# State-space stage of a five-layer model: decaying the state's part of y by rows of y, instead of scaling C for each head

## The chip, the cores and the metric

The kernel runs on one core of a Trainium2 chip. The metric is the device time of one execution in microseconds; the median of several runs is given. Everything is in float32.

## The reference, what matters of it

The model takes 1024 tokens of 512 features and adds six layers to them, one after the other, each behind a layer norm:

```python
x = x + 0.5 * ffn0(ln(x))        # 8 experts, top 2
x = x + attention(ln(x))         # 32 heads
x = x + 0.5 * ffn0(ln(x))
x = x + 0.5 * ffn1(ln(x))        # 4 routed LoRA adapters of rank 8
x = x + state_space(ln(x))       # the layer that is changed
x = x + 0.5 * ffn1(ln(x))
```

The state-space layer has 64 heads of 64 channels. The heads form 8 groups of 8; a group shares its vectors B and C of 128 elements (the state's width). From a projection of the input and a convolution over 4 tokens come x, B and C, from another projection the gate, and from a third the step dt of each head and token. Then, for each head (64 channels p, 128 state elements n):

```python
state = state * dA_t + (dt_t * x_t)[:, None] * B_t[None, :]   # dA = exp(-exp(A_log) * dt)
y_t   = state @ C_t
...
y  = y + x * D
yn = y * rsqrt(mean(y * y over the group's 512 channels) + eps) * norm_weight * silu(gate)
out = yn @ out_proj.T
```

## The kernel before, in words

The layers run one after another in one program. TensorE's (PE's) work is written out in program order; the tile framework adds semaphores and lets each engine (PE; VectorE, DVE; ScalarE, ACT; GpSimd, POOL; SyncE, SP, which issues most DMAs) run its own instructions in an order that it fixes when the program is built. [...] What buffers there are decides how far one engine can run ahead: `psml`, four PSUM tiles of one bank (`ps_y`, `ps_st`, `ps_tr`, `ps_ss`, `ps_out` and others take turns in it); `pbig`, two for the projections `ps_in`; in SBUF `ep`, two buffers of each of `dd`, `e_seg` and `cs`; `w2`, two of each of `xdt`, `xw`, `y`, `sq`, `yg`, `state`; `wpool`, four for weights.

The state-space layer is `mamba`. The scan over tokens is done in chunks of 128 tokens, 8 of them. First `steps_of_time` works out dt for every head and token (tiles `dt_e`, `dt_u` and so on, L1044 and L1047 among them), and writes two sets of rows to the DRAM tile `decay`: row 0 holds the decay dA of each token, row 1, `ecum`, the decay from the chunk's start to each token. SBUF tiles `erev` and `etot` hold the decay from each token to the chunk's end, and over the whole chunk.

Then come 16 units: 8 groups times two halves of 512 tokens, each half of four chunks. `load_group` loads a group's weights `w_bc`, `w_x`, `w_g` and `w_out`. For each chunk i of a unit the loop does, in program order:

1. `scan(un, i)`: this chunk's outputs and the new state.
2. projections for the **next** unit (`project_pair`, matmuls at L230): at i = 0 those of B, C and half of x (16 matmuls), at i = 1 the other half of x (8) and `finish_bc` (transposes of B, and `ps_bc` = C against B, masked to `gt`), at i = 2 and 3 the gate (8 each, `w_g`). The convolution of x, B and C takes six DVE instructions a tile, L1161 and L1170, so chunks 0 and 1 are DVE's heavy ones.
3. `prepare` for the next chunk.
4. `project_out` for this chunk.

`prepare` loads `dd`, two broadcasts of 1024 decay values (8 heads of 128 tokens) to all 128 partitions, 512 KB each. DVE makes from row 0 the decays between all pairs of tokens of a chunk by a scan (`e_seg`, L1265), and multiplies them by `gt` (L1273). PE transposes x (`ps_tr`, L156); DVE scales it by dt (`xdt`, L1278), and POOL that by `erev` (`xw`, L1284). For all chunks but a sequence's first (56 of 64), POOL also makes `cs`: C, which has the state's 128 elements on partitions, times row 1, for each of the 8 heads (128 x 1024, L1290).

`scan` forms `ps_y`, with the group's 512 channels as 4 blocks of 128 partitions by 128 tokens; a head's 64 channels are the lower or upper half of the partitions of a block. Eight matmuls with 64 columns of weights (`xdt` of one head) against `e_seg` of that head give the part from the chunk's own tokens, and eight more (the head's `state` against its `cs`) add the state's part in the same bank (both L1308). DVE adds `xd`, which is x times D (`y_m`, L1317). ACT squares y (`sq`, L1321), and DVE multiplies y by the gate (`yg`, L1323). The state goes on by `ps_st` (L1326), POOL's `state` times `etot` (L1333) and a DVE add (L1336). POOL adds the four blocks of squares in two steps (L1340, L1341), except in the last unit.

`project_out` sums the squares over partitions (`ps_ss`, L1349: one matmul, four in the last unit), makes the scale `ss` (L149 on DVE, L150 on POOL), multiplies `yg` by the output weights (`ps_out`, four matmuls, L1360), and adds that to x (L1363).

In the last group `after.step()` mixes in tiles of the last layer. In the last unit there are no projections left to stand between `scan` and `project_out`.

Of the kernel before, what the change touches and what calls it, by code (L numbers as in the profile page):

```python
# [13 lines left out]
F32 = mybir.dt.float32  # L14
# [4 lines left out]
ALU = mybir.AluOpType  # L19
# [3 lines left out]
P = 128  # L23
# [17 lines left out]
MP = 64  # L41
# [3 lines left out]
HPG = MH // MG  # L45
# [30 lines left out]
def macaron_kernel(  # L76
# [23 lines left out]
    nc = tc.nc  # L100
# [5 lines left out]
    psml = ctx.enter_context(tc.tile_pool(name="psml", bufs=4, space=PSUM))  # L106
# [6 lines left out]
    decay = [  # L113
        dram.tile([NCH // 2, 2, MH * P], F32, tag=f"decay{q}", name="decay")
        for q in range(2)
    ]
# [35 lines left out]
    def transposes(src, n):  # L152

        ps = psml.tile([P, 512], F32, tag="ps", name="ps_tr")
        for i in range(n):
            nc.tensor.transpose(ps[:, i * P : (i + 1) * P], src(i), ident)  # L156
        return ps
# [849 lines left out]
    def mamba(lora, par):  # L1007
        conv, dsk, nwt, w_dt, dtb, av = par.conv, par.dsk, par.nwt, par.w_dt, par.dtb, par.av
        nct = MI // P
        with ExitStack() as ms:  # L1010
# [13 lines left out]
            with tc.tile_pool(name="m_dt", bufs=1) as dp, tc.tile_pool(  # L1024
                name="m_pair", bufs=3
# [99 lines left out]
            w2 = ms.enter_context(tc.tile_pool(name="m_w2", bufs=2))  # L1125
            ep = ms.enter_context(tc.tile_pool(name="m_e", bufs=2))
            heads = [P, HPG, MP]

            def as_heads(a):
                return a.rearrange("p (h d) -> p h d", d=MP)  # L1130
# [51 lines left out]
            def begin_unit(gr, hf):  # L1182
                g = gr["g"]
                un = {"gr": gr, "hf": hf, "g": g, "last": (g, hf) == (MG - 1, 1)}
                un["bT"] = bp.tile([P, half], F32, tag="bT", name="bT")
                un["cT"] = bcp.tile([P, half], F32, tag="cT", name="cT")
                un["btok"] = bcp.tile([P, 4, P], F32, tag="btok", name="btok")
                un["gt"] = bcp.tile([P, 4, P], F32, tag="gt", name="gt")
                un["xc"] = bcp.tile([P, 4, half], F32, tag="xc", name="xc")
                un["xd"] = bcp.tile([P, 4, half], F32, tag="xd", name="xd")  # L1190
                un["sg"] = bcp.tile([P, 4, half], F32, tag="sg", name="sg")
                return un
# [56 lines left out]
            def per_head(a, un, i):  # L1249
                c, h0 = 4 * un["hf"] + i, un["g"] * HPG  # L1250
                return a[:, c, h0 : h0 + HPG].unsqueeze(2).to_broadcast(heads)

            def prepare(un, i):

                c, h0 = 4 * un["hf"] + i, un["g"] * HPG
                tok = slice(i * P, (i + 1) * P)
                dd = ep.tile([P, 2, HPG * P], F32, tag="dd", name="dd")
                for q in range(2):
                    nc.sync.dma_start(
                        dd[:, q, :],  # L1260
                        decay[un["hf"]][i, q, h0 * P : (h0 + HPG) * P].partition_broadcast(P),
                    )

                e = ep.tile([P, HPG, P], F32, tag="e", name="e_seg")
                nc.vector.tensor_tensor_scan(  # L1265
                    e.rearrange("p h l -> p (h l)"),
                    dd[:, 0, :],
                    eye8.rearrange("p h l -> p (h l)"),
                    0.0,
                    ALU.mult,  # L1270
                    ALU.add,
                )
                nc.vector.tensor_tensor(  # L1273
                    e, e, un["gt"][:, i, :].unsqueeze(1).to_broadcast([P, HPG, P]), ALU.mult
                )
                ps = transposes(lambda k: un["xc"][:, k, tok], 4)
                xdt = w2.tile([P, D], F32, tag="xdt", name="xdt")
                nc.vector.tensor_tensor(  # L1278
                    as_heads(xdt), as_heads(ps), per_head(dtp, un, i), ALU.mult
                )  # L1280
                xw = None
                if c < NCH - 1:
                    xw = w2.tile([P, D], F32, tag="xw", name="xw")
                    nc.gpsimd.tensor_tensor(  # L1284
                        as_heads(xw), as_heads(xdt), per_head(erev, un, i), ALU.mult
                    )
                cs = None
                if c > 0:
                    cs = ep.tile([P, HPG, P], F32, tag="cs", name="cs")
                    nc.gpsimd.tensor_tensor(  # L1290
                        cs,
                        un["cT"][:, tok].unsqueeze(1).to_broadcast([P, HPG, P]),
                        dd[:, 1, :].rearrange("p (h l) -> p h l", l=P),
                        ALU.mult,
                    )
                return e, xdt, xw, cs

            def scan(un, i, e, xdt, xw, cs):

                c, gr = 4 * un["hf"] + i, un["gr"]  # L1300
                tok = slice(i * P, (i + 1) * P)
                before = gr["state"]
                py = psml.tile([P, 512], F32, tag="ps", name="ps_y")
                terms = [(xdt, e)] + ([(before, cs)] if before is not None else [])
                for n, (left, right) in enumerate(terms):
                    for h in range(HPG):
                        r0 = (h % 2) * MP
                        nc.tensor.matmul(  # L1308
                            py[r0 : r0 + MP, (h // 2) * P : (h // 2 + 1) * P],
                            lhsT=left[:, h * MP : (h + 1) * MP],  # L1310
                            rhs=right[:, h, :],
                            start=(n == 0 and h < 2),
                            stop=True,
                            skip_group_check=not (n == 0 and h < 2),
                        )
                y = w2.tile([P, 4, P], F32, tag="y", name="y_m")
                nc.vector.tensor_tensor(  # L1317
                    y, py.rearrange("p (k l) -> p k l", l=P), un["xd"][:, :, tok], ALU.add
                )
                sq = w2.tile([P, 4, P], F32, tag="sq", name="sq")  # L1320
                nc.scalar.activation(sq, y, AF.Square)  # L1321
                yg = w2.tile([P, 4, P], F32, tag="yg", name="yg")
                nc.vector.tensor_tensor(yg, y, un["sg"][:, :, tok], ALU.mult)  # L1323
                if c < NCH - 1:
                    pst = psml.tile([P, 512], F32, tag="ps", name="ps_st")
                    nc.tensor.matmul(  # L1326
                        pst, lhsT=un["btok"][:, i, :], rhs=xw, start=True, stop=True
                    )
                    st = w2.tile([P, D], F32, tag="state", name="state")
                    if before is None:  # L1330
                        nc.vector.tensor_copy(st, pst)
                    else:
                        nc.gpsimd.tensor_tensor(  # L1333
                            as_heads(st), as_heads(before), per_head(etot, un, i), ALU.mult
                        )
                        nc.vector.tensor_tensor(st, st, pst, ALU.add)  # L1336
                    gr["state"] = st
                n = 4
                if not un["last"]:
                    nc.gpsimd.tensor_tensor(sq[:, :2, :], sq[:, :2, :], sq[:, 2:, :], ALU.add)  # L1340
                    nc.gpsimd.tensor_tensor(sq[:, 0, :], sq[:, 0, :], sq[:, 1, :], ALU.add)  # L1341
                    n = 1
                return un, c, yg, sq, n
# [26 lines left out]
            un = begin_unit(gr, 0)  # L1370
            for j in range(5):
                project_pair(un, j)
                if j == 1:
                    finish_bc(un)
            ready = prepare(un, 0)
            plan = ((0, 1), (2,), (3,), (4,))
            for n, _ in enumerate(units):
                nxt = None
                if n + 1 < len(units):
                    g, hf = units[n + 1]  # L1380
# [22 lines left out]
                un = nxt  # L1403
# [74 lines left out]
```

## Time and profile before

| | before |
|---|---|
| runs | 2933.84, 2933.5, 2931.63 us |
| median of the runs | 2933.5 us |
| profiled execution, own time | 2935.3 us |
| its span | 2933.6 us |
| mean granted TensorE clock | 0.978 |
| TensorE (PE) busy | 2800.9 us, 95% |
| VectorE (DVE) busy | 1745.8 us, 60% |
| GpSimd (POOL) busy | 898.8 us, 31% |
| ScalarE (ACT) busy | 709.4 us, 24% |
| `cs`, L1290, on POOL | 56 instructions, 184.2 us |

The span is that of the slowest (here the only) core in the profiled execution; its own time is a little longer, since it holds what lies around the span. Busy times of engines overlap, so they don't add up to the span. The state-space layer with what is mixed into it takes about the last third, from some 1876 to 2900 us. A line number stands for a line of the kernel before, unless it is said to be of the changed kernel.

### The profile page before, as it was taken

What the parts mean: (1) busy time and instruction counts of PE and PEld (TensorE: products, weight loads), DVE (VectorE), ACT (ScalarE), POOL (GpSimd) and SP (SyncE); (2) the same over time, 40 slices, a digit from 0 to 9 for tenths busy, and PEclk for the clock granted to TensorE, in tenths of its full rate; (3) what the DMA queues carried; (4) which work ended last, traced back from release to release, by engine and by line L of the source; (5) the groups of instructions that cost most, each with busy time, mean ns of one, the idle gap of its engine ahead of it and who ended that gap; (6) DMA issues with size and microseconds to landing.
All of it is one profiled execution on the core that took longest, in us unless ns stands there. A gap on an engine that the chain in (4) does not pass through costs nothing.

```text
span 2933.6 us, 30294 instructions
## 1 busy us (share of the span) xinstructions
PE 2800.9 (95%) x11051; PEld 1587.3 (54%) x11051; DVE 1745.8 (60%) x3239; ACT 709.4 (24%) x1381; POOL 898.8 (31%) x733
## 2 busy tenths in 40 slices
PE   5979999999999999999999769899999999999989
PEld 3435666656666666666654334454555555555544
DVE  3146555665656656556564234777776777767673
ACT  1212212231212222212222222422222232222320
POOL 4231112121122212112100230255554545455450
PEclk8989999999999999999999889999999999999999
DMA  8420001010010001001015340233232222223210
GB/s 297 126 72 29 15 15 44 1 44 15 15 44 15 29 15 43 15 15 43 1 36 194 101 122 18 83 101 108 86 108 94 86 98 97 93 87 122 87 44 29
DMA packets 102178, 196.99 MB, mean 67 GB/s; under 512 B 9040, under 2 KB 34800, under 8 KB 102032
## 3 DMA queue, kind: packets, MB, share of 16 engines
q1 hardware_dynamic: 84896, 157.15, 16.1%
q0 software_dynamic: 6240, 20.45, 2.7%
q10 hardware_dynamic: 10896, 17.47, 1.6%
q8 instruction: 89, 1.46, 0.2%
q14 instruction: 57, 0.47, 0.1%
HBM read 176.17 MB, written 18.87 MB: 66 GB/s over the span
## 4 chain that ended last, share of the span: by engine, by line
PE 84%; DVE 6%; POOL 4%; issue 3%; DMA 2%; ACT 0%; POOLq 0%; DVEq 0%; SPq 0%; ACTq 0%
PE ps_in L230 15%; PE ps_m L912 13%; PE ps_o L732 8%; PE ps_s L708 8%; PE ps_tr L156 7%; PE ps_out L1360 6%; PE ps_m L884 6%; PE ps_wo L821 6%; PE ps_e L510 5%; PE ps_y L1308 3%; PE ps_up L241 2%; PE ps_st L1326 1%; DVE xc L1161 1%; DVE e_seg L1265 1%; PE ps_v L241 1%
## 5 line engine op out<-in xcount | busy, mean ns | idle before, releaser
L708 PE MATMUL ps_s<-kT,qT 128*128 128x512 f32 (+3 forms) x768 | 292.8, 488 | 0.1
L732 PE MATMUL ps_o<-pT,v 128*128 128x512 f32 (+3 forms) x768 | 260.4, 489 | 0.0
L753 ACT COPY pT<-ps_tr 128x256 f32<-128x256 f32 (+2 forms) x192 | 91.7, 478 | 647.3 <-PE ps_tr L156 635.5
L722 ACT ACTIVATE pr<-ps_s,nm 128x128 f32<-128x128 f32 (+7 forms) x256 | 190.3, 744 | 238.3 <-DVE nm L719 207.9
L1360 PE MATMUL ps_out<-w_out,yg 128*128 128x512 f32 x512 | 241.1, 615 | 3.0 <-DVE yg L1323 3.0
L230 PE MATMUL ps_in<-hT,w_g 128*128 128x512 f32 x512 | 227.1, 596 | 8.2 <-issue 8.2
L1290 POOL TENSOR_TENSOR cs<-cT,dd 128x1024 f32<-128x1024 f32 x56 | 184.2, 3289 | 161.6 <-PE ps_y L1308 138.8
L230 PE MATMUL ps_in<-hT,w_x 128*128 128x512 f32 x512 | 225.8, 593 | 0.0
L732 PEld LDWEIGHTS ps_o<-pT,v 128*128 128x128 f32 x768 | 144.3, 191 | 145.6 <-issue 99.9
L719 DVE TENSOR_REDUCE nm<-ps_s 128x1 f32<-128x128 f32 (+7 forms) x256 | 192.2, 752 | 3.9
L156 PEld LDWEIGHTS ps_tr<-ident,pr 128*128 128x128 f32 x1152 | 136.9, 142 | 76.1 <-issue 44.8
L156 PE MATMUL ps_tr<-ident,pr 128*128 128x128 f32 x1152 | 171.4, 276 | 4.5 <-DVE pr L724 3.2
L510 PE MATMUL ps_e<-w_all,xt_s 128*128 (+1 forms) x368 | 168.1, 601 | 0.0
L724 DVE TENSOR_SCALAR pr<-pr,sm 128x128 f32<-128x128 f32 (+7 forms) x256 | 162.9, 637 | 7.7 <-DVE sm L723 0.5
L230 PEld LDWEIGHTS ps_in<-hT,w_g 128*128 128x128 f32 x512 | 96.6, 190 | 127.8 <-issue 127.8
L230 PEld LDWEIGHTS ps_in<-hT,w_x 128*128 128x128 f32 x512 | 97.0, 190 | 120.9 <-issue 120.4
L1265 DVE TENSOR_TENSOR_SCAN e_seg<-dd,eye 128x1024 f32<-128x1024 f32 x64 | 152.3, 2380 | 7.7 <-PE ps_y L1308 5.8
L1161 DVE SCALAR_TENSOR_TENSOR xc<-ps_in,conv,xc 128x511 f32<-128x511 f32 (+2 forms) x192 | 141.5, 737 | 17.9 <-ACT xc L1157 17.6
L708 PEld LDWEIGHTS ps_s<-kT,qT 128*128 128x128 f32 x768 | 127.5, 192 | 39.8 <-issue 26.8
L1360 PEld LDWEIGHTS ps_out<-w_out,yg 128*128 128x128 f32 x512 | 94.5, 195 | 98.4 <-issue 98.4
L806 POOL TENSOR_TENSOR so<-oT 128x256 f32<-128x256 f32 x28 | 20.0, 726 | 380.2 <-DVE oT L739 336.7
L1284 POOL TENSOR_TENSOR xw<-xdt,erev 128x512 f32<-128x512 f32 x56 | 58.4, 1043 | 251.6 <-DVE xdt L1278 195.0
(271 smaller groups left out, 4759.2 us busy)
## 6 DMA issues: line engine op xcount, KB each, us to landing
dd<-decay SPq DMA_DIRECT2D x128, 512.0 KB
w_all<-in_w_e_dram SPq DMA_DIRECT2D x16, 1024.0 KB
outs<-y_e ACTq DMA_DIRECT2D x46, 256.0 KB
w_v<-in_wkv_dram SPq DMA_DIRECT2D x8, 1024.0 KB
w_q<-in_wq_dram SPq DMA_DIRECT2D x32, 256.0 KB
w_k<-in_wkv_dram SPq DMA_DIRECT2D x8, 1024.0 KB
w_o<-in_wo_dram SPq DMA_DIRECT2D x8, 1024.0 KB
w_x<-in_in_wt_dram SPq DMA_DIRECT2D x8, 1024.0 KB
```

The source lines that it names most:

```text
L156: nc.tensor.transpose(ps[:, i * P : (i + 1) * P], src(i), ident)
L230: nc.tensor.matmul(ps[:, cols : cols + n], lhsT=w[:, k, c0 : c0 + P], rhs=hT[:, k, t0 : t0 + n], start=(k == 0), stop=(k == KT - 1),)
L510: nc.tensor.matmul(ps, lhsT=xt[:, k, :], rhs=w_all[:, bass.ds(ep, 1), k, :].rearrange("p e c -> p (e c)"), start=(k == 0), stop=(k == KT - 1),
L708: nc.tensor.matmul(ps[:, j : j + m], lhsT=qT[:, qt * P : (qt + 1) * P], rhs=kT[:, j : j + m], start=True, stop=True,)
L719: nc.vector.tensor_reduce(nm, ps[:, :n], AX.X, ALU.max, negate=True)
L722: nc.scalar.activation(pr[:, :n], ps[:, :n], AF.Exp, bias=nm, accum_out=sm)
L732: nc.tensor.matmul(ps[:, lo:512], lhsT=v[:, kb, hh * P : (hh + 1) * P], rhs=pT[:, kb, lo:512], start=(kb == 0), stop=(kb == last),)
L821: nc.tensor.matmul(ps[:, j, :], lhsT=lf[i][k][:, j * P : (j + 1) * P], rhs=rt[i][:, k, :], start=(first and j == 0 and k == 0), stop=(k == 1),
L912: nc.tensor.matmul(ps, lhsT=gr["left"][i][:, k, hh * P : (hh + 1) * P], rhs=right[i][:, k, :], start=(first and k == 0), stop=(last and k ...
L1265: nc.vector.tensor_tensor_scan(e.rearrange("p h l -> p (h l)"), dd[:, 0, :], eye8.rearrange("p h l -> p (h l)"), 0.0, ALU.mult, ALU.add,)
L1290: nc.gpsimd.tensor_tensor(cs, un["cT"][:, tok].unsqueeze(1).to_broadcast([P, HPG, P]), dd[:, 1, :].rearrange("p (h l) -> p h l", l=P), ALU ...
L1360: nc.tensor.matmul(po, lhsT=yg[:, k, :], rhs=w_o[:, k, :], start=(k == 0), stop=(k == 3))
```

## The change

A head's decay does not depend on the state's elements, so it can be applied to the result for each channel and token as well as to C. The changed kernel does that:

- `prepare` loads only row 0 into `dd`. For chunks behind a sequence's first, row 1 goes into a new tile `ec` of 128 partitions by 4 blocks by 128 tokens, laid out as y is: two broadcasts to 64 partitions, one for the even and one for the odd heads, 128 KB each in pieces of 512 bytes. `cs` and its POOL instruction are gone.
- `scan` forms the state's part by four matmuls with 128 columns of weights (`state` of two heads) against C itself, in a bank of its own, `ps_z` (L1318 of the changed kernel). DVE multiplies it by `ec` into a new tile `z_m` (L1326), POOL adds `xd` to that in place (L1329), and DVE adds `ps_y` and `z_m` (L1332). In a sequence's first chunk y is `ps_y` plus `xd`, as before.

```diff
-                dd = ep.tile([P, 2, HPG * P], F32, tag="dd", name="dd")
-                for q in range(2):
-                    nc.sync.dma_start(
-                        dd[:, q, :],
-                        decay[un["hf"]][i, q, h0 * P : (h0 + HPG) * P].partition_broadcast(P),
-                    )
+                dd = ep.tile([P, HPG * P], F32, tag="dd", name="dd")
+                nc.sync.dma_start(
+                    dd, decay[un["hf"]][i, 0, h0 * P : (h0 + HPG) * P].partition_broadcast(P)
+                )
+
+                ec = None
+                if c > 0:
+                    ec = ep.tile([P, 4, P], F32, tag="ec", name="ec")
+                    src = decay[un["hf"]][i, 1, h0 * P : (h0 + HPG) * P].rearrange(
+                        "(k r l) -> r k l", r=2, l=P
+                    )
+                    for r in range(2):
+                        nc.sync.dma_start(
+                            ec[r * MP : (r + 1) * MP, :, :], src[r].partition_broadcast(MP)
+                        )
...
-                cs = None
-                if c > 0:
-                    cs = ep.tile([P, HPG, P], F32, tag="cs", name="cs")
-                    nc.gpsimd.tensor_tensor(
-                        cs,
-                        un["cT"][:, tok].unsqueeze(1).to_broadcast([P, HPG, P]),
-                        dd[:, 1, :].rearrange("p (h l) -> p h l", l=P),
-                        ALU.mult,
-                    )
-                return e, xdt, xw, cs
...
                 py = psml.tile([P, 512], F32, tag="ps", name="ps_y")
-                terms = [(xdt, e)] + ([(before, cs)] if before is not None else [])
-                for n, (left, right) in enumerate(terms):
-                    for h in range(HPG):
-                        r0 = (h % 2) * MP
+                for h in range(HPG):
+                    r0 = (h % 2) * MP
+                    nc.tensor.matmul(
+                        py[r0 : r0 + MP, (h // 2) * P : (h // 2 + 1) * P],
+                        lhsT=xdt[:, h * MP : (h + 1) * MP],
+                        rhs=e[:, h, :],
+                        start=(h < 2),
+                        stop=True,
+                        skip_group_check=h >= 2,
+                    )
+                more = un["xd"][:, :, tok]
+                if before is not None:
+                    pz = psml.tile([P, 512], F32, tag="ps", name="ps_z")
+                    for k in range(4):
                         nc.tensor.matmul(
-                            py[r0 : r0 + MP, (h // 2) * P : (h // 2 + 1) * P],
-                            lhsT=left[:, h * MP : (h + 1) * MP],
-                            rhs=right[:, h, :],
-                            start=(n == 0 and h < 2),
+                            pz[:, k * P : (k + 1) * P],
+                            lhsT=before[:, k * P : (k + 1) * P],
+                            rhs=un["cT"][:, tok],
+                            start=True,
                             stop=True,
-                            skip_group_check=not (n == 0 and h < 2),
                         )
+                    z = w2.tile([P, 4, P], F32, tag="z", name="z_m")
+                    nc.vector.tensor_tensor(
+                        z, pz.rearrange("p (k l) -> p k l", l=P), ec, ALU.mult
+                    )
+                    nc.gpsimd.tensor_tensor(z, z, more, ALU.add)
+                    more = z
                 y = w2.tile([P, 4, P], F32, tag="y", name="y_m")
                 nc.vector.tensor_tensor(
-                    y, py.rearrange("p (k l) -> p k l", l=P), un["xd"][:, :, tok], ALU.add
+                    y, py.rearrange("p (k l) -> p k l", l=P), more, ALU.add
                 )
```

More of the change, by code (lines that the diff above doesn't have):

```diff
@@ L1266, in prepare @@
                     e.rearrange("p h l -> p (h l)"),
-                    dd[:, 0, :],
+                    dd,
                     eye8.rearrange("p h l -> p (h l)"),
@@ L1286, in prepare, with scan @@
                     )
-                cs = None
-                if c > 0:
-                    cs = ep.tile([P, HPG, P], F32, tag="cs", name="cs")
-                    nc.gpsimd.tensor_tensor(
-                        cs,
-                        un["cT"][:, tok].unsqueeze(1).to_broadcast([P, HPG, P]),
-                        dd[:, 1, :].rearrange("p (h l) -> p h l", l=P),
-                        ALU.mult,
-                    )
-                return e, xdt, xw, cs
-            def scan(un, i, e, xdt, xw, cs):
+                return e, xdt, xw, ec
+            def scan(un, i, e, xdt, xw, ec):
                 c, gr = 4 * un["hf"] + i, un["gr"]
```

## The prediction

> **What bounds the kernel now.** I read the profile page first (its span, its line of busy times, its groups), then the windows of the state-space stage, then PE's timeline for the order and the cadence of the matmuls, then the waits, and last the timelines of POOL and DVE at the places where PE waits.
>
> ```profile
> span 2933.6 us, 30294 instructions
> PE 2800.9 (95%) x11051; PEld 1587.3 (54%) x11051; DVE 1745.8 (60%) x3239; ACT 709.4 (24%) x1381; POOL 898.8 (31%) x733
> ...
> L1290 POOL TENSOR_TENSOR cs<-cT,dd 128x1024 f32<-128x1024 f32 x56 | 184.2, 3289 | 161.6 <-PE ps_y L1308 138.8
> ```
>
> TensorE is busy 95% of the span. The product `cs` that the change drops is the longest elementwise operation on POOL, 56 times 3.3 us, but POOL is busy for only 31%. The windows view (start and end, then sum and busy time of PE, PEld, DVE, ACT and POOL, granted clock, DMA share) of 200 us inside the state-space stage:
>
> ```profile
> 2200.00:2400.00 200.00, 199.37 (x842) 101.72 (x841) 142.49 (x196) 54.36 (x80) 98.32 (x67) 1.00 0.28 95
> ```
>
> PE idles 0.63 us in 200 us, at a granted clock of 1.00. So the 184 us of `cs` aren't on the path: the change can gain only where PE's own work shrinks, at the few places where PE waits, and at the edges of the stage.
>
> **PE's own work.** The timeline gives the starts (start, duration); the second pair is `finish_bc`, four 128x128 matmuls of 128 columns, the very shape of the new `ps_z`.
>
> ```profile
> 2307.59 1.09 PE L1308 MATMUL ps_y<-e_seg,xdt 128*64 128x128 f32 x16
> 2308.51 1.04 PE L1308 MATMUL ps_y<-cs,state 128*64 128x128 f32 x16
> 2309.48 1.13 PE L1326 MATMUL ps_st<-xw,btok 128*128 128x512 f32 x2
> 2310.45 1.02 PE L230 MATMUL ps_in<-hT,w_g 128*128 128x512 f32 x2
> ...
> 2352.45 1.06 PE L1239 MATMUL ps_bc<-cT,bT 128*128 128x128 f32 x8
> 2353.34 0.60 PE L156 MATMUL ps_tr<-ident,xc 128*128 128x128 f32 x4
> ```
>
> The state's part costs little for 8 matmuls: 0.97 us from its start to that of `ps_st` (the 64-wide ones run in pairs, one in each half of the array). From the start of `ps_y` to the next projection it is now 2310.45 − 2307.59 = 2.86 us. After: `ps_y` 0.92, or 1.02 where a 128-wide matmul follows (2003.05 to 2004.07 in a chunk without a state part); `ps_z` 2353.34 − 2352.45 = 0.89; `ps_st` 0.97, or 0.86 if the 0.1 for passing from 64 to 128 wide has been paid at `ps_z`. That makes 2.77 to 2.88. I take 2.83, −0.03 a chunk, over 56 chunks **−1.7 us** (bounds 56 × −0.09 = −5.0 and 56 × 0.01 = +0.6).
>
> **The places where PE waits.** The waits view (waiter, releaser: us, count, mean) names one steady wait inside the stage, and the timelines show it at the first two chunks of each group's conv half:
>
> ```profile
> PEld ps_ss L1349 <- POOL sq L1341: 8.0, 15, 0.6
> ```
> ```profile
> 2025.02 2.36 POOL L1290 TENSOR_TENSOR cs<-cT,dd 128x1024 f32<-128x1024 f32 x1 [1.51 <-PE ps_y L1308]
> ...
> 2025.65 1.74 DVE L1170 SCALAR_TENSOR_TENSOR xc<-hist,conv,xc 128x2 f32<-128x2 f32 x1
> ...
> 2028.10 0.68 DVE L1317 TENSOR_TENSOR y_m<-ps_y,xd 128x512 f32<-128x512 f32 x1
> ...
> 2030.84 2.70 POOL L1340 TENSOR_TENSOR sq<-sq 128x256 f32<-128x256 f32 x1
> 2033.62 1.32 POOL L1341 TENSOR_TENSOR sq<-sq 128x128 f32<-128x128 f32 x1
> 2035.00 0.38 PE L1349 MATMUL ps_ss<-ones,sq 128*128 128x1 f32 x2 [0.38 <-POOL sq L1341]
> ...
> 2046.93 2.02 POOL L1333 TENSOR_TENSOR state<-state,etot 128x512 f32<-128x512 f32 x1
> ...
> 2049.42 0.38 PE L1349 MATMUL ps_ss<-ones,sq 128*128 128x1 f32 x2 [0.24 <-POOL sq L1341]
> ```
>
> With the bubbles beside them, the two places cost 0.64 and 0.50 us of PE, 1.14 a group, 8.0 in seven groups (the eighth is mixed with the last FFN).
>
> Site one after: `cs` is gone, so the two-column L1170, 1.74 long here and 0.21 elsewhere, gives back 1.53. The new chain puts `z` (0.68, the price of L1317, which also reads PSUM), a hop of 0.09 (`xdt` to `xw`) and POOL's add (1.04, the price of `xw`, 128x512) ahead of `y`: 1.81. So `y` starts 0.28 later. `state×etot` (1.36 here) now starts when the add ends, 2028.4, and the squares' sums at 2029.8 instead of 2030.84; even at their long 2.70 + 1.32 they end by 2033.9, ahead of the 2034.62 at which PE would want them. The wait goes: −0.64.
>
> Site two after: here `y` (2044.21) is later by the full 1.81, so the squares (ACT, 0.63) are ready at about 2047.5. `cs` no longer stands before them, but `state×etot` (1.04 to 2.02) runs from 2046.0 to 2047.1 or 2048.0, and the sums (1.17 + 0.45 in this place) end at 2049.1 to 2049.7 against 2049.4 now. I take +0.15. Together −0.49 × 7 = **−3.5 us** (bounds: both waits gone, −8.0; site two at 2.5 times today's cost while site one stays, about +6). In the other chunks the sums end at 2315.70 where PE wants them at 2317.64, so 1.9 us are spare; `y` takes 1.1 of it, since `e*gt` (2.73 beside `cs`, 1.21 elsewhere) gives the rest back, and 0.8 is left. If that cover were gone, each 0.1 us beyond it would cost 3 us over some 30 chunks.
>
> **The start of the stage.** The two first `cs` run on POOL from 1843.09 to 1849.86, beside the chain that makes dt, while PE idles 8.21 us until 1855.85. The tile view of `dt_u` (count: min/mean/max ns):
>
> ```profile
> L1044 DVE TENSOR_SCALAR dt_u<-dt_e x2: 284/1009/1734, 1820.8 to 1845.9; 128x256 f32<-128x256 f32 x2
> ```
>
> One instance is 1.734 beside `cs` and 0.284 without; its neighbour L1047 has 1.770 and 0.293. That is −2.9 on an unbroken DVE chain. Against it, SP issues two `ec` transfers ahead of the first `dd`, 0.42 each, on which the first scan waits; the second 512 KB transfer is gone. I take **−2.5** (bounds −2.9 and +1). Later in the stage one 512 KB load gives way to two of 128 KB; a `dd` is asked for about a chunk ahead and the DMA engines are 28% busy, so I cost the extra 48 issues at nothing; a pair is 0.84 us on SP, and the weights and the next `dd` queued behind it hold PE up nowhere now (0.63 us idle of 200, above); should the cover be gone, it is up to 0.84 us for each of 56 chunks.
>
> **The tail.** In the last unit no projections cover `y`:
>
> ```profile
> 2875.50 0.69 DVE L1317 TENSOR_TENSOR y_m<-ps_y,xd 128x512 f32<-128x512 f32 x1 [1.99 <-PE ps_y L1308]
> ...
> 2876.91 1.05 PE L1349 MATMUL ps_ss<-ones,sq 128*128 128x1 f32 x8
> ```
>
> PE takes up the squares as soon as ACT has them. The chain of 1.81 is bare in its last two chunks, +3.6; in the first two `yg` loses a 2.73 us `e*gt` ahead of it and they come out even; the rest of group 7 I put at +0.5. Sum **+4.2** (bounds +2 and +7).
>
> **Sum.** −2.5 − 1.7 − 3.5 + 4.2 = −3.5. All durations are from one profiled execution of 2935.3 us (span 2933.6), 1.8 above the median of the runs, 2933.5; the sum makes it 2931.8, and the median 2930.0.
>
> [...] POOL's elementwise rows depend on the company: `state×etot` has 2.02 above and 1.04 in another chunk:
>
> ```profile
> 2316.06 1.04 POOL L1333 TENSOR_TENSOR state<-state,etot 128x512 f32<-128x512 f32 x1 [0.36 <-DVE state L1336]
> ```
>
> [...]
>
> **The rivals.** *Both waits go, and PE's part reaches its lower bound.* For it: the squares' sums lose `cs` as their neighbour everywhere. Then −2.9 − 5.0 − 8.0 + 4.2 = −11.7: 2921.8 us. Against it: site two's arithmetic above. Chance 0.29. *Slower: the add on POOL sits inside DVE's in-order queue.* `y` waits for it, and scan, `yg`, `e*gt` and the conv steps are queued behind `y`. If it takes 2.02, as `state×etot` did beside DVE work, instead of 1.04, that is 0.98 at 2 places in 7 groups, +13.7, and +2.0 in the tail, on −3.5: +12.2, 2945.7 us. An excess of 0.22 (a mean of 1.26) brings the sum to zero, one of 0.59 (1.63) to 5.9 slower. For it: the 2.02, 1.36 and 2.70 rows; against it: those met DVE operations on two SBUF tiles. Chance 0.28. *PE's part halves*, if eight matmuls become four at half the pair's cost: 56 × −0.44 = −24.6, 2909 us; against it the `ps_bc` row, 0.89 for just such four. Chance 0.03.
>
> **How the numbers follow.** 0.2%, 5.9 us, is about what a measurement of this kernel can tell from no change. The main case has 0.40, its own range 2926 to 2937: no change. Faster is the first rival and the third, 0.32; slower is the second, 0.28. The range takes in the first rival at 2921 and the second at 2947; outside stay the halved PE and the far sides of both.
>
> **What would show it.** Right: `ps_z` at 0.89 and 2.8 us from `ps_y` to the projection; L1044 and L1047 near 0.29; `z` (L1326) at 0.68, the add (L1329) near 1.04; no wait of `ps_ss` at site one, one of about 0.4 at site two; longer waits in the last unit. Wrong: an add above 1.3, waits of `ps_ss` in the w_g chunks or of PE on `e_seg`, `ps_y` waiting for scan.

## The result, and the profile after

| | before | after |
|---|---|---|
| median of the runs | 2933.22 us (8 runs) | 2943.36 us (8 runs) |
| profiled execution: its span | 2933.6 us | 2941.0 us |

The ratio is 1.0034, with a 95% interval of 1.0023 to 1.0045: slower by 10 us (7 to 13). The forecast was 2930, no change. The time lies inside the range that the prediction gave, but beyond the 0.2% that it called no change, and on the side of its second rival.

The page of the kernel after, with the new add on POOL among its groups:

```profile
span 2941.0 us, 29456 instructions
...
PE 2803.0 (95%) x10603; PEld 1590.2 (54%) x10603; DVE 1736.9 (59%) x3295; ACT 709.0 (24%) x1381; POOL 763.6 (26%) x733
...
L1329 POOL TENSOR_TENSOR z_m<-z_m,xd 128x512 f32<-128x512 f32 x56 | 77.3, 1381 | 288.9 <-DVE z_m L1326 282.9
```

POOL has lost 135 us of work and DVE 9, and the kernel is slower. The add takes 1.38 us on average, where the sum had 1.04.

Where the time went is seen by setting the starts of `ps_out` in the two timelines, one for each chunk, against each other:

| place | before | after | difference | step |
|---|---|---|---|---|
| projection ahead of PE's wait for dt | 1840.50 | 1835.77 | −4.73 | |
| first `ps_out` of the stage | 1892.20 | 1885.56 | −6.64 | −1.9 |
| the same chunk seven groups later | 2782.24 | 2778.45 | −3.79 | +2.9 |
| end of the unit ahead of the last | 2828.27 | 2825.86 | −2.41 | +1.4 |
| last `ps_out` of the last unit | 2897.20 | 2904.08 | +6.88 | +9.3 |
| end of the span | 2933.6 | 2941.0 | +7.4 | +0.5 |

The rows of the last unit, before and then after, the first of each five being the end of the unit ahead of it:

```profile
2828.27 3.68 PE L1360 MATMUL ps_out<-w_out,yg 128*128 128x512 f32 x8
2841.32 6.14 PE L1360 MATMUL ps_out<-w_out,yg 128*128 128x512 f32 x8 [1.42 <-DVE yg L1323]
2860.40 5.14 PE L1360 MATMUL ps_out<-w_out,yg 128*128 128x512 f32 x8 [1.57 <-DVE yg L1323]
2877.83 3.68 PE L1360 MATMUL ps_out<-w_out,yg 128*128 128x512 f32 x8
2897.20 5.38 PE L1360 MATMUL ps_out<-w_out,yg 128*128 128x512 f32 x8
```
```profile
2825.86 3.68 PE L1375 MATMUL ps_out<-w_out,yg 128*128 128x512 f32 x8
2840.03 5.47 PE L1375 MATMUL ps_out<-w_out,yg 128*128 128x512 f32 x8
2860.07 5.38 PE L1375 MATMUL ps_out<-w_out,yg 128*128 128x512 f32 x8
2879.93 5.38 PE L1375 MATMUL ps_out<-w_out,yg 128*128 128x512 f32 x8
2904.08 5.86 PE L1375 MATMUL ps_out<-w_out,yg 128*128 128x512 f32 x8
```

The −4.73 ahead of the stage is in code that the change doesn't touch; in the eleven traces of this case the same projection starts anywhere from 1835.77 to 1840.50, and at 1840.26 in the kernel that had only its first unit changed (below). I count it as scatter between executions, which is why the two spans differ by less than the medians. The steps below it add up to +12.1 (7.4 + 4.73), of which the last unit, counted to the end of the span, makes 9.8.

The start of the stage came as forecast in this pair of traces. The tile view of `dt_u`, after:

```profile
L1044 DVE TENSOR_SCALAR dt_u<-dt_e x2: 285/286/288, 1816.0 to 1841.7; 128x256 f32<-128x256 f32 x2
```

Both instances are at 0.29 now. PE's wait there goes from 8.21 to 5.76 us. That the size fits the forecast of −2.5 so well is in part luck: in the nine traces here with the new form in the first unit the wait is 5.21 to 7.46 us, in the two without it 8.21 and 8.46.

PE's own work, from the timeline of the kernel after (a chunk of the last unit, where nothing is cut off):

```profile
2873.32 1.09 PE L1306 MATMUL ps_y<-e_seg,xdt 128*64 128x128 f32 x16
2874.34 1.16 PE L1318 MATMUL ps_z<-cT,state 128*128 128x128 f32 x8
2875.34 1.02 PE L1341 MATMUL ps_st<-xw,btok 128*128 128x512 f32 x2
2876.20 0.60 PE L156 MATMUL ps_tr<-ident,xc 128*128 128x128 f32 x4
2879.01 1.05 PE L1364 MATMUL ps_ss<-ones,sq 128*128 128x1 f32 x8 [2.22 <-ACT sq L1336]
2879.93 5.38 PE L1375 MATMUL ps_out<-w_out,yg 128*128 128x512 f32 x8
```

`ps_y` 1.02, `ps_z` 1.00, `ps_st` 0.86 make 2.88 against 2.86 before: +0.02 a chunk. The waits view, stage alone, after and then before:

```profile
PEld ps_ss L1364 <- ACT sq L1336: 13.6, 4, 4.0
PEld ps_ss L1364 <- POOL sq L1356: 10.5, 16, 1.1
```
```profile
PEld ps_ss L1349 <- ACT sq L1321: 5.6, 4, 2.0
```

The first line is the last unit alone, four chunks, 8.0 us more than before. The second is the wait of the earlier groups, 10.5 against 8.0.

At what the prediction called site two, the timelines of DVE, POOL and PE show the new chain whole:

```profile
2037.51 0.68 DVE L1326 TENSOR_TENSOR z_m<-ps_z,ec 128x512 f32<-128x512 f32 x1
...
2038.27 1.26 POOL L1329 TENSOR_TENSOR z_m<-z_m,xd 128x512 f32<-128x512 f32 x1 [1.46 <-DVE z_m L1326]
...
2039.57 0.69 DVE L1332 TENSOR_TENSOR y_m<-ps_y,z_m 128x512 f32<-128x512 f32 x1 [0.78 <-POOL z_m L1329]
...
2043.11 0.38 PE L1364 MATMUL ps_ss<-ones,sq 128*128 128x1 f32 x2 [0.83 <-POOL sq L1356]
```

From the start of `z` to that of `y` it is 2039.57 − 2037.51 = 2.06, and PE's wait at `ps_ss` has grown from 0.24 to 0.83. Site one has no wait any more (−0.63 a group), site two costs 0.60 more, the third chunk of each group's second half has a new one of 0.25, and PE's own work 0.02 in each of seven chunks: +0.36 a group, 2.5 in seven; the table has 2.9 with what the last group's edge adds.

### The profile page after: what moved, and what is told of

The parts are those of the page before. It is cut to its first block, busy times and chain, and to the rows that moved or that the text cites. A ratio compares the mean times of both kernels' runs of the same rounds, so it can differ in the third digit from the quotient of the medians.

```text
span 2941.0 us, 29456 instructions
## 1 busy us (share of the span) xinstructions
PE 2803.0 (95%) x10603; PEld 1590.2 (54%) x10603; DVE 1736.9 (59%) x3295; ACT 709.0 (24%) x1381; POOL 763.6 (26%) x733
## 4 chain that ended last, share of the span: by engine, by line
PE 83%; DVE 7%; POOL 4%; issue 3%; DMA 2%; ACT 1%; POOLq 0%; SPq 0%; DVEq 0%; ACTq 0%
PE ps_in L230 14%; PE ps_m L912 13%; PE ps_o L732 8%; PE ps_s L708 8%; PE ps_tr L156 6%; PE ps_out L1375 6%; PE ps_m L884 6%; PE ps_wo L821 6%; PE ps_e L510 5%; DVE xc L1161 2%; PE ps_up L241 2%; PE ps_y L1306 2%; PE ps_z L1318 1%; PE ps_st L1341 1%; PE ps_v L241 1%
## 5 line engine op out<-in xcount | busy, mean ns | idle before, releaser
L1329 POOL TENSOR_TENSOR z_m<-z_m,xd 128x512 f32<-128x512 f32 x56 | 77.3, 1381 | 288.9 <-DVE z_m L1326 282.9
L708 PEld LDWEIGHTS ps_s<-kT,qT 128*128 128x128 f32 x768 | 127.5, 192 | 39.8 <-issue 26.8
L518 DVE TENSOR_TENSOR y_e<-ps_e,b_all 128x512 f32<-128x512 f32 x46 | 31.8, 692 | 166.9 <-PE ps_e L510 146.2
```

What stands on the lines that cost most here:

```text
L708: nc.tensor.matmul(ps[:, j : j + m], lhsT=qT[:, qt * P : (qt + 1) * P], rhs=kT[:, j : j + m], start=True, stop=True,)
```

## The experiments

Ratios are to the kernel before, run on the same chip.

**The last unit put back.**

```diff
+ un["fresh"] = not un["last"]      # in begin_unit
...
+ if c > 0 and not fresh:           # in prepare: row 1 loaded whole into cs
+     nc.gpsimd.tensor_tensor(cs, un["cT"][:, tok].unsqueeze(1).to_broadcast([P, HPG, P]), cs, ALU.mult)
...
+ if before is not None and not un["fresh"]:   # in scan: eight matmuls (state, cs) into ps_y
```

> Only the last unit (group 7, second half) goes back to the form of before: row 1 is broadcast whole, POOL scales C for each head, eight 64-wide matmuls add into ps_y. All else is the changed kernel. Theory L (the loss lies in the last unit, where nothing covers y: by the traces ps_out there starts 9.8 us later against before than at the end of the unit ahead of it): 2943.4 - 9.8 = 2933.6 us, within 3 of the kernel before. Rival S (the POOL add in DVE's in-order queue costs in every group): the loss stays, 2940 us or more. Rival E (the loss comes from outside the stage): no change, 2943.

Measured: 2931.46, ratio 0.9996 (0.9986 to 1.0005). The loss is gone. A caution on its size: the old form in this kernel isn't quite the kernel before, since row 1 is loaded into `cs` itself and multiplied in place. By its trace the last unit is 5 us shorter than in the kernel before: `ps_out` hardly waits for `yg` there (0.19 us twice, 1.42 and 1.57 before, where `e*gt` stood ahead of `yg`), and one `ps_out` takes 3.68 us instead of 5.38. The groups keep the loss of the change (127.5 us each instead of 127.15), and the 5 us make up for it.

**Only the last unit changed.** The same code with the condition turned round.

> The kernel before, with only the last unit in the changed form. Theory L: 2933.2 + 9.8 = 2943 us. Rival S: 2933 to 2935. Rival E: as before, 2933. If both this kernel and the one with the last unit put back agree with L, the other 15 units together are worth less than 3 us either way.

Measured: 2944.71, ratio 1.0038 (1.0025 to 1.0052). With one unit of sixteen changed the kernel is as slow as with all. By its trace the unit itself is 7.7 us longer than in the kernel before; the waits of `ps_ss` on ACT there are 13.8 us, as in the full change (13.6). The other 1.7 us of the difference in spans lie ahead of it.

**The add on DVE.**

```diff
-                    nc.gpsimd.tensor_tensor(z, z, more, ALU.add)
+                    nc.vector.tensor_tensor(z, z, more, ALU.add)
```

> The changed kernel with z += xd on DVE instead of POOL, in the same place between z and y. The add is 1.26 us on POOL where nothing runs beside it, with 0.14 to it and 0.04 back; on DVE I expect 0.7 to 1.0. Theory L with the price of the add as cause: 0.5 to 0.7 less in each chunk of the last unit, and shorter waits leave PE's clock higher, -3 to -5 there; in the first seven groups the wait at the second chunk (1.09 us) falls to about 0.6, -3.5. Together 2935 to 2938 us. Rival: DVE is the bound in the conv chunks, another 0.7 in its queue shows as new waits of ps_ss in each group, and the time stays at 2943 or rises.

Measured: 2949.48, ratio 1.0049 (1.0036 to 1.0063), where I had expected 2935 to 2938: no gain; by the medians a further loss, though the intervals overlap. The add takes 0.68 us there, half of what it takes on POOL, but the DVE timeline shows what else moved:

```profile
2043.17 0.68 DVE L1329 TENSOR_TENSOR z_m<-z_m,xd 128x512 f32<-128x512 f32 x1
2043.78 2.06 DVE L1282 TENSOR_TENSOR e_seg<-e_seg,gt 128x1024 f32<-128x1024 f32 x1
2045.76 0.68 DVE L1332 TENSOR_TENSOR y_m<-ps_y,z_m 128x512 f32<-128x512 f32 x1
```

In the built order `e*gt` now stands between the add and `y`, which starts 3.78 us behind `z` (2041.98), where the changed kernel has 2.06. Site two costs 1.35 more than before in each group. So this run doesn't say what the add's place costs; it says what an operation of 2 us ahead of `y` costs. My theory's number failed here, since it left the order out.

**The add first.**

```diff
+                nc.vector.tensor_tensor(y, py.rearrange("p (k l) -> p k l", l=P), un["xd"][:, :, tok], ALU.add)
                 if before is not None:
...
-                    nc.gpsimd.tensor_tensor(z, z, more, ALU.add)
+                    nc.vector.tensor_tensor(y, y, z, ALU.add)
```

> The changed kernel with the two adds in another order: DVE makes y = ps_y + xd while PE still works on ps_z, then z = ps_z times ec, then y += z, all on DVE; nothing on POOL. The chain behind ps_z is z (0.68) and one add of two SBUF tiles (0.7 to 1.0) against z, hop, 1.26, hop, y (0.69) in the changed kernel: 1.2 to 1.5 us shorter. Theory L: the last unit loses 4 to 6 us, the waits at the second chunk of each group go back to about those of before (-0.6 a group, -4): 2933 to 2936 us. Rival (the bound is PE's slower ps_z and not the chain): 2941 or more.

Measured: 2928.94, ratio 0.9981 (0.9972 to 0.9990): faster than the kernel before, by some 15 us faster than the change, and below the 2933 to 2936 that I had expected. Its windows view in the middle of the stage:

```profile
2200.00:2400.00 200.00, 199.99 (x773) 102.42 (x773) 151.70 (x221) 56.05 (x83) 65.94 (x56) 1.00 0.22 71
```

PE does not wait at all in these 200 us, though DVE has 9 us more to do than before. `ps_z` is the same in this kernel; so it was the chain, not PE's form of the product, that cost. Two things changed at once here, the order of the adds and the engine of one of them.

**Half the add.**

```diff
-                    nc.gpsimd.tensor_tensor(z, z, more, ALU.add)
+                    nc.gpsimd.tensor_tensor(z[:, :2, :], z[:, :2, :], more[:, :2, :], ALU.add)
```

> The changed kernel with POOL's add for two of the four blocks of channels only (xd is left out of the other two): 128x256 instead of 128x512, about 0.65 instead of 1.26 us alone. Theory L with the add's length as price: the wait at the second chunk of each group falls from 1.09 by about 0.6 (-4 in seven groups), the last unit by 0.6 a chunk and some of PE's slow rows (-3 to -4): 2935 to 2937. Rival (not the length but the passage to another engine and back costs): less than 2 us gained, 2941 or more.

This kernel leaves `xd` out of half of y, so it serves for its time alone. Measured: 2931.62, ratio 0.9986 (0.9977 to 0.9995), where I had expected 2935 to 2937. The tile view gives the add's length here, 728 ns in the median; in the kernel after it is 1268:

```profile
L1329 POOL TENSOR_TENSOR z_m<-z_m,xd x56: 722/728/1634, 1897.6 to 2890.5; 128x256 f32<-128x256 f32 x56
```
```profile
L1329 POOL TENSOR_TENSOR z_m<-z_m,xd x56: 1260/1268/2182, 1893.5 to 2899.7; 128x512 f32<-128x512 f32 x56
```

With 0.54 us less in the chain, same engine and same two passages, the steady waits are gone (`ps_ss` waits 1.5 us on POOL in the whole stage, where the kernel after has 10.5; a group is 0.86 shorter than before, instead of 0.36 longer: 8.5 us in seven groups), and the last unit costs 5.4 us instead of 9.8. The length of the add decides the sign of the change.

**PE kept busy in the last unit.** Extra matmuls, not read by anyone, stand between the transposes and `ps_ss`.

```diff
+                    if un["last"]:
+                        pf = pbig.tile([P, S], F32, tag="pb", name="ps_fill")
+                        for _ in range((8, 6, 4, 7)[i]):
+                            nc.tensor.matmul(pf[:, :512], lhsT=ident, rhs=un["xd"][:, 0, :], start=True, stop=True)
                     project_out(*done)
```

> The changed kernel with 8, 6, 4 and 7 extra matmuls (identity against xd, 128 by 512, result never read) in the four chunks of the last unit, where PE waits for the squares; 0.43 us each, so that they fill most of the 3.9, 3.3, 2.4 and 3.6 us of waiting there. Theory C (part of the last unit's loss is that PE runs slower after it has waited: ps_ss 1.73 us instead of 0.91, ps_out 5.21 and 5.70 instead of 3.61): with PE kept busy these go back to about 0.91 and 3.61, -4 to -6 us, 2938 to 2939. Rival (the slower rows have another cause, or the chain through DVE and POOL ends last anyway): 2943, or above it by what the filling delays.

Measured: 2939.59, ratio 1.0018 (1.0009 to 1.0027). The expectation had the wrong length for a filling matmul: four take 3.43 us, 0.86 each. So the filling was longer than the wait that it covers in every chunk (6.87 us against 3.77 in the first, 6.01 against 3.58 in the last), and the kernel still came out lower than the change, with intervals that overlap a little. The windows view shows why, by its clock column. The stretch behind the squares in the third chunk, and behind the last, for the kernel after:

```profile
2881.90:2883.50 1.60, 1.60 (x3) 0.68 (x2) 0.00 (x0) 0.00 (x0) 0.00 (x0) 0.50 0.00 0
...
2902.35:2904.08 1.73, 1.73 (x8) 1.73 (x9) 0.01 (x1) 0.00 (x0) 0.00 (x0) 0.50 0.00 0
```

and the same places with the filling:

```profile
2879.70:2884.10 4.40, 4.40 (x18) 2.42 (x17) 0.16 (x1) 0.00 (x0) 0.55 (x1) 1.00 0.00 0
2903.50:2908.00 4.50, 4.50 (x18) 2.52 (x17) 0.16 (x1) 0.00 (x0) 0.55 (x1) 1.00 0.00 0
```

After the waits the granted clock is 0.50 in these stretches, and `ps_out` takes 5.38 us in the third chunk and 5.86 in the last; with PE kept at work the clock is 1.00 in both, and `ps_out` takes 3.68 in both.

**A shorter filling.** The same with (4, 3, 2, 4).

> The filling again with 4, 3, 2 and 4 extra matmuls: in the run before, one of them took 0.86 us (two passes of 0.43), so that the filling itself was longer than the wait in the first and the last chunk of the unit. Theory C: the wait for the squares then ends shortly after the filling, ps_ss takes about 0.9 and ps_out about 3.6 in all four chunks, and nothing is delayed: 2936 to 2938 us, another 2 to 3 less than with the long filling. Rival (the gain of the long filling had another cause): 2939 to 2943.

Measured: 2938.07, ratio 1.0017 (1.0008 to 1.0026), at the upper edge of what was expected and not to be told from the longer filling. The built order put one or two of the matmuls behind `ps_ss` or ahead of the chunk, so that in the last chunk only one stood in the wait; there PE waited 2.71 us more, and `ps_out` took 6.19. In the third chunk, where the wait was mostly filled, it took 3.60. How much of the time the clock is worth by itself stays open by these times (4 to 5 us, the two kernels against the change, with overlapping intervals); that it is lost behind waits, and kept by the filling, is shown by the clock column (0.50 against 1.00).

**The first unit alone changed.** The hybrid with `un["fresh"] = (g, hf) == (0, 0)`.

> The kernel before, with only the very first unit (group 0, first half) in the changed form, so that POOL does not scale C while DVE works out dt for the second half of the tokens. Theory: L1044 and L1047 take 0.3 us each instead of 1.75 and the projection behind them starts 2.3 us earlier, as in the changed kernel's trace: 2930 to 2931 us. Rival (the gain there belongs to other differences between the two profiled executions): 2933, no change.

Measured: 2932.9, ratio 0.9989 (0.9980 to 0.9998), 3 us (1 to 6) below the kernel before on the same chip; the median is not within the 2930 to 2931 expected. By its trace PE's wait for dt is 5.50 us instead of 8.21. But the time doesn't show this gain by itself: the units in the old form, with `cs` multiplied in place, differ too. From the first `ps_out` to the same chunk seven groups later this kernel takes 3.9 us more than the kernel before, and in the last unit some 3.6 less. What speaks for the gain are the waits for dt in all eleven traces, above.

**The add first, and the last unit as before.** Both edits together.

> The order with the add first (y = ps_y + xd, then z, then y += z, all on DVE) in all units but the last, and the form of before in the last. Theory: the add-first kernel gains up to the last group and gives back 3.5 us in the last unit by its trace; with the old form there it keeps them: 2925 to 2926.5 us, against 2928.9 and 2932.3 for the kernel before. Rival (mixing two forms costs in the rotation of buffers at the unit's edge): 2929 or more.

Measured: 2920.67, ratio 0.9954 (0.9940 to 0.9967): 13 us faster than the kernel before, and more than the 2925 to 2926.5 expected. It beats both kernels. By its trace 4.8 us are won in seven groups, and some 7 in the last unit, which in this form (`cs` multiplied in place) is shorter than in the kernel before.

## Why the prediction was wrong

The terms of the sum against what the two traces show:

| term | forecast | measured |
|---|---|---|
| start of the stage | −2.5 | −2.5 at PE's wait (8.21 to 5.76) |
| PE's own work, 56 chunks | −1.7 | +1.1 |
| waits in seven groups | −3.5 | about +1.5: 7 × (−0.63 + 0.60 + 0.25) |
| the tail | +4.2 | +11.2: last unit 9.8, the rest of the last group 1.4 |

*The first step that failed is the price of POOL's add*, "POOL's add (1.04, the price of `xw`, 128x512)". It is 1.26 where it runs alone, 1.27 in the median and 1.38 on average. `xw` and `state×etot` have the same shape in the row, but their second operand is one value per head, spread over 64 columns; the add reads two full tiles. The rows print the tile's shape, not how an operand is spread, and I took the nearest shape. (They also multiply where this one adds; no run here tells the two apart.) The attention layer has POOL rows with two full operands in the trace before, one of them of the very shape:

```profile
L787 POOL TENSOR_TENSOR to<-w_o,to 128x512 f32<-128x512 f32 x14 | 17.8, 1271 | 0.5
```

L806, 128x256, takes 0.73 there, the length of the halved add. With the two passages (0.07 to 0.14, and 0.02 to 0.04 back) the chain from `z` to `y` is 2.06 in most chunks and 2.04 to 2.13 in the last unit, for a forecast of 1.81. At site two +0.15 became +0.60: against PE's `ps_tr`, `y` comes 2.26 later than before instead of 1.81, 0.25 of that by the chain and 0.20 because `z` starts later than `y` did, and the two sums of squares take 2.06 together instead of 1.62. In the other chunks the spare time of 0.8 held in all but one of each group.

The right price alone would not have changed the forecast: 0.22 at the 16 places that the second rival counts is +3.5, which brings the sum from −3.5 to 0. What made the kernel slower is above all the tail.

*The larger miss is the tail, +4.2 for +11.2.* The forecast said the chain of 1.81 is bare in the last two chunks and comes out even in the first two. The waits of `ps_ss` grew in all four, by 8.0 us together; 3.0 of it comes back, since `ps_out` no longer waits for `yg` in the first two. That is +5.0, of which the forecast had 3.6. The rest wasn't in it at all: PE runs at half its clock in more places of the unit, in `ps_ss` (1.73 instead of 0.91, twice, at a granted clock of 0.50, behind waits of 3.77 and 3.58), `ps_out` (four slow ones instead of three) and `ps_y` and `ps_z` of the second chunk (1.91 and 1.21 instead of 1.02 and 1.00, at a granted clock of 0.51, behind a wait for `zm` of 1.79 that is as long in the trace before, where `ps_y` isn't slow). That is some 4.5 us by these rows. The trace before had the signs: `ps_out` in the last unit at 6.14, 5.14 and 5.38, and 3.68 in the chunk where nothing waited.

The add takes 1.27 us on POOL, in the median, and 0.68 in the run that has it on DVE: 1.86 times as long. On POOL its length differed with what DVE did beside it: the add takes 1.26 beside the state add, which reads PSUM, and 1.26 with DVE idle. Seven adds, one a group, take 2.17 to 2.18 us; they stand in the last chunk of a sequence, where the built order has `e*gt` (two SBUF tiles) right behind `z`.

*The second rival had the right instruction and the right side, but not the places.* It put 14 of its 16 places in the seven groups and two in the tail; the runs have 2.5 us in seven groups and 9.8 in the last unit. It put the turning point at a mean of 1.26 and "5.9 slower" at 1.63. At the measured mean of 1.38 its law gives about +2, and that mean is raised by the seven adds of 2.18, which cost nothing where they stand (13.08 us from the `ps_out` ahead to that of their chunk, against 13.06 before). The half-add run shows the slope to be larger than it said, some 12 to 14 us for 0.54 us of length, where 16 places of the rival give 8.6.

*PE's own work* was mis-sized by 0.05 a chunk: I took 0.89 for `ps_z` from `ps_bc`, which follows matmuls of the same width; here it takes 1.00 up to `ps_st`, and `ps_st` then takes the 0.86 of its lower bound. It is the upper end of the range given, 2.88, which is +0.02 a chunk and +1.1 in all, where the prediction has 0.01 and +0.6. Two more slips of 0.1 in its sums (−0.49 × 7 is −3.4, and 2 × 1.81 + 0.5 is 4.1) move nothing.

*What was right*: the 184 us of `cs` on POOL were worth nothing on the path; the start of the stage, by its cause; site one; no wait on the new transfers (PE shows none on `ec`, and none of more than 0.2 us on a weight).

## What to carry to other kernels

The 184 us of `cs` taken off POOL, which was busy for 31% of the span, bought 2.5 us at the start of the stage and 0.63 in each group, where DVE had been slow beside it, and the 2.06 us put into the chain cost nearly their whole length where nothing covered it (8.0 us more of waits in four chunks): look for the last iteration of a pipelined loop and price it by itself. Take a duration from a row that matches in operands, spread or full, and not in tile shape alone (here 1.04 in the row taken, 1.27 for the add and for L787). When a product is split into two sums, let the add that needs only the early operand run while the late one is still being made; here that, with the add on DVE, turned +10 us into −5; the add on DVE in its old place gained nothing.

## What the runs showed of the hardware that was not expected

PE's lower clock does not follow from the length of the wait alone. Behind a wait of 2.22 us on ACT in the third chunk of the last unit `ps_out` took 5.38 us in the changed kernel (the rows are above; the granted clock was 0.50 in the middle of it), and 3.68 behind the same 2.22 us in the kernel with only the last unit changed:

```profile
2883.79 1.05 PE L1388 MATMUL ps_ss<-ones,sq 128*128 128x1 f32 x8 [2.22 <-ACT sq L1360]
2884.70 3.68 PE L1399 MATMUL ps_out<-w_out,yg 128*128 128x512 f32 x8
```

Behind 1.52 us in the last chunk it took 5.38 in the kernel before, at a granted clock of 0.67 over that stretch, and 3.68 with the last unit put back, at 1.00. What else it follows, no run here shows. A consequence for reading: behind one and the same wait a `ps_out` can take 1.7 us more or not, so a difference of that size at one place of one trace need not come from the edit.
